# Graph convolutions: the last targets summed from gathered rows instead of a table product

## The chip, the cores and the metric

The kernel runs on one core of one Trainium2 chip. The metric is the device time of one execution in microseconds. Before the change it is 4117.46 us, the median of three runs (4089.36, 4117.46, 4130.27).

The engines are called as the profile calls them: PE (TensorE, products), DVE (VectorE), ACT (ScalarE), POOL (GpSimd) and SP (SyncE). Each executes its own instructions in their written order and waits for other engines and transfers by semaphores. Transfers are issued on the queues of SP and ACT; transfers with indirect addresses (gathers and scatters by row numbers) are issued on POOL.

## The reference

3125 nodes with 256 features, 50,000 edges sorted by target. Eight stages follow one another, and each adds to `x` what it makes of its layer-normed rows:

```python
x = x + gnn0(ln(x), edges)   # attention, 4 heads
x = x + ffn0(ln(x))          # 8 experts, top 2
x = x + gnn1(ln(x), edges)   # two attention layers
x = x + ffn1(ln(x))          # a recurrence over the rows
x = x + gnn2(ln(x), edges)   # three graph convolutions
x = x + ffn2(ln(x))          # 8 experts of width 1024, top 2
x = x + gnn3(ln(x), edges)   # one graph convolution
x = x + ffn3(ln(x))          # 8 experts of width 512, top 2
```

The change touches the convolutions of `gnn2` and `gnn3`. One layer of `gnn2` is

```python
h = h @ W
agg = segment_sum(h[src] * norm[:, None], dst)   # self loops are among the edges
h = relu(agg + b)                                # no relu after the third layer
```

with `norm = d[src] * d[dst]`, `d` the degree to the power -1/2. `gnn3` is one such layer without self loops, bias and relu.

## The kernel before, in words

**Tiles.** Nodes are cut into 25 tiles of 128 (NT = 25, padded to NP = 3200). An early part of the kernel builds a table of edges: for each pair (source tile, target tile) a 128x128 block of counts. A convolution is then dense: for each target tile, the sum over the 25 source tiles of a product of the block with the sources' rows `hs` (scaled by `d`). The blocks lie in DRAM (`ct`) as bf16, and `hs` is split into three bf16 parts (high, mid, low; `parted`, L840: two casts on POOL, L847 and L849, two differences on DVE, L848 and L850, per two tiles).

**Layers.** `gcn` (L1585) runs a whole stage. `gnn2` has three layers. The front norms `x`, multiplies by the first weight and writes `hs`. Layers 0 and 1 go through `convolve` (L1529): spans of up to four target tiles (`even_spans(4)`: seven spans, 4,4,3,4,3,4,3 tiles), and per span 25 sources x 2 halves x 3 parts = 150 products with the block as the moving operand (L1540, 128x512 or 128x384). The sums of a span lie in two PSUM tiles, with two sets of them (`accp`), and `done` takes them: DVE multiplies by the targets' `d` (L1663), ACT adds the bias with relu (L1664), PE multiplies by the next weight (L369) in what is already the next span's time, ACT scales (L1656), and `parted` makes the next `hs`. The last layer, and `gnn3`, goes through `convolve_rows` (L1546): spans of two targets, and per source and target a pair of products, L1560 (128x512: high and mid part) and L1564 (128x256: low). DVE adds the sums to `x` (L1684).

**The blocks' loads.** `table_columns` (L814) loads the blocks of one span in groups of source tiles on SP's queue (L822) into three rotating buffers (`cpool`). With self loops, POOL adds the identity to a diagonal block as soon as its group has landed (L828, `c<-c,ident`); PE's products on that block wait for it.

**The experts' fronts.** While `convolve_rows` goes on, tiles whose `x` is complete pass through the front of the next experts (`Experts.front`, L2202): norm on DVE, transposes and the gate's product on PE, choice and places on DVE (L2240 and after), again small products on PE (L2262, L2263), then two scatters of rows per tile on POOL (`slots`, L2348). `ready` gives the pieces lags in steps (a step is one target tile), and the loop writes them between the products. After CERTAIN = 20 tiles sent, `load_ahead` (L2400) starts loads for the experts.

**Order.** Within an engine the order of instructions is fixed at build time by a scheduler, which plans with its own costs of instructions. `with tc.issue_after(i)` tells it that what is written inside comes behind `i`; the engines of the two matter, as the order below shows. Gathers as such are used before the change in the attention stages only (L2023, one gather of 128 rows per 128 edges).

**Stages in time**, by the trace: up to 930 us the table, `gnn0` and its experts; 930 to 1757 `gnn1`; 1757 to 1827 the projection of the recurrence; 1827 to 2480 the recurrence; 2500 to 2755 front and layer 0 of `gnn2`; 2755 to 2984 layer 1; 2984 to 3206 the rows layer; 3206 to 3615 the experts of width 1024; 3615 to 3879 `gnn3` (rows from 3656); to the end the last experts.

The functions that the change touches, with the profile's line numbers:

## Time and profile before

| | us |
|---|---|
| median of three runs | 4117.46 |
| the profiled execution's own time | 4123.68 |
| its span in the profile | 4121.8 |
| PE busy | 3555.9 (86%) |
| DVE busy | 2155.3 (52%) |
| POOL busy | 1401.9 (34%) |
| ACT busy | 1212.7 (29%) |
| mean clock granted to PE | 0.913 of full speed |

Busy time per stage (us; DMA is the mean busy share of the 16 DMA engines):

| stretch | length | PE | DVE | POOL | DMA |
|---|---|---|---|---|---|
| 1757–1827 projection | 70 | 69.0 | 36.7 | | |
| 2500–2755 front and layer 0 | 255 | 249.3 | 57.8 | 46.4 | 0.26 |
| 2755–2984 layer 1 | 229 | 228.1 | 28.6 | 27.2 | 0.32 |
| 2984–3174 rows | 190 | 188.5 | 111.3 | 44.2 | 0.57 |
| 3206–3615 experts | 409 | 388.6 | | | |
| 3670–3879 rows of gnn3 | 209 | 206.2 | 91.6 | 38.7 | 0.52 |

How to read it: the busy share of PE is an average over the stages. In the attention stages POOL and DVE are busy too; from 2500 us on, PE is the only engine that is busy nearly all the time. In a list of events each row has start, length, engine, line, operation, `out<-in`, and in brackets the idle time of the engine before it and what ended it. In a list of waits, "who waited for it" names the engines that stood idle until the instruction was done.

### The profile page before, as it was taken

The numbers are of one execution on the slowest core, as the hardware profiler recorded it, in microseconds if no ns is written. First come the engines' busy times: TensorE is split into PE (matmuls) and PEld (weight loads), VectorE is DVE, ScalarE is ACT, GpSimd is POOL, SyncE is SP. The second block draws the span as 40 slices with busy tenths as digits, with TensorE's granted clock in tenths as the row PEclk, the third lists the DMA queues.
The fourth block names the chain that finished last, engine by engine and source line by source line (L and its number), as shares of the span: only waits on it lengthen the run. The fifth ranks groups of instructions, "written<-read, shape, count | busy, mean of one in ns | idle before, by whom it ended". The sixth has DMA issues, their size and how long they took to land. (4 is left out here: it accounts for less than half of the span.)

```text
span 4121.8 us, 72442 instructions
## 1 busy us (share of the span) xinstructions
PE 3555.9 (86%) x25990; PEld 2149.1 (52%) x26079; DVE 2155.3 (52%) x7897; ACT 1212.7 (29%) x4041; POOL 1401.9 (34%) x1321
## 2 busy tenths in 40 slices
PE   4567878676878868899999998999999999989988
PEld 3233222463222356675454455555566788856677
DVE  7567788646766645557677675111156411153411
ACT  2455333434333302114444444000100322330122
POOL 2756666444767357400000003111122222222243
PEclk8666887798989979999999999999999999989999
DMA  4444432563333254300000002333364444445465
GB/s 123 136 137 143 141 105 79 142 223 109 107 105 108 73 156 140 87 3 2 2 2 2 2 2 61 88 94 92 91 197 143 144 117 117 122 129 157 134 158 122
DMA packets 366387, 422.32 MB, mean 102 GB/s; under 512 B 44076, under 2 KB 320864, under 8 KB 362295
## 3 DMA queue, kind: packets, MB, share of 16 engines
q1 hardware_dynamic: 286833, 260.46, 21.0%
q0 software_dynamic: 62224, 140.41, 13.1%
q10 hardware_dynamic: 16950, 16.54, 1.2%
q8 instruction: 219, 3.59, 0.4%
q14 instruction: 161, 1.32, 0.1%
HBM read 337.37 MB, written 82.62 MB: 102 GB/s over the span
## 5 line engine op out<-in xcount | busy, mean ns | idle before, releaser
L2023 POOL DMA_INDIRECT edge<-scored,from x720 | 830.6, 1154 | 517.9 <-issue 238.9
L1540 PE MATMUL acc<-c,hs 128*128 128x512 bf16 (+1 forms) x2069 | 405.9, 356 | 1.7 <-POOL hs L847 0.2
L1801 PE MATMUL pz<-lstm_v,hist 128*32 128x192 f32 x7120 | 382.5, 333 | 19.3 <-DVE hist L1906 7.3
L1560 PE MATMUL acc<-hs,c 128*128 128x512 bf16 x1192 | 394.9, 379 | 0.0
L2689 PE MATMUL ph<-xt,first 128*128 128x256 f32 (+1 forms) x1624 | 351.1, 371 | 5.7 <-ACT xt L2655 3.1
L1564 PE MATMUL acc<-hs,c 128*128 128x256 bf16 x1250 | 340.6, 272 | 3.0
L2707 PE MATMUL py<-w,ht 128*128 x1484 | 337.8, 382 | 4.5 <-issue 4.1
L2082 ACT ACTIVATE edge<-edge,factor 128x65 f32<-128x65 f32 (+1 forms) x960 | 251.3, 349 | 218.8 <-DVE factor L2077 170.4
L2689 PEld LDWEIGHTS ph<-xt,first 128*128 128x128 f32 x1624 | 290.6, 196 | 41.3 <-ACT xt L2655 5.4
L1540 PEld LDWEIGHTS <-hs 128*128 128x128 bf16 x2100 | 205.6, 98 | 199.2 <-POOL hs L847 0.6
L2707 PEld LDWEIGHTS py<-w,ht 128*128 128x128 f32 x1484 | 282.9, 192 | 43.6 <-issue 5.2
L976 DVE SCALAR_TENSOR_TENSOR v<-q,g1ahv,c 128x384 f32<-128x384 f32 (+1 forms) x400 | 240.4, 646 | 112.0 <-remote 52.3
L1837 PE MATMUL pz<-pre,ident 128*128 128x192 f32 x900 | 268.4, 381 | 12.1 <-PEq L1914 11.6
L1801 PEld LDWEIGHTS pz<-lstm_v,hist 128*32 128x32 f32 x7120 | 186.0, 109 | 167.7 <-DVE hist L1906 135.9
L2348 POOL DMA_INDIRECT slots<-rows,sloti x150 | 168.5, 1123 | 307.5 <-DVE rstd L345 136.7
L2697 ACT ACTIVATE ht<-ph,first 128x256 f32<-128x256 f32 (+1 forms) x406 | 160.8, 456 | 323.2 <-PE ph L2689 284.3
L681 PE MATMUL pa<-hi,lo 128*128 128x350 bf16 (+2 forms) x600 | 166.4, 422 | 96.8 <-ACT cols L688 40.4
L1611 POOL TENSOR_TENSOR disc<-deg,expo 128x25 f32<-128x25 f32 x1 | 4.4, 4360 | 714.6 <-DVE ends L1911 714.6
L1131 PE MATMUL acc<-g1bhv,v 128*128 128x257 f32 x850 | 218.0, 407 | 25.2 <-issue 9.9
L1884 ACT ACTIVATE z<-pz 128x128 f32<-128x128 f32 (+1 forms) x900 | 176.5, 248 | 198.1 <-PE pz L1801 197.5
L2092 PE MATMUL edgeacc<-edge,hot 128*32 128x264 f32 (+1 forms) x1440 | 152.3, 468 | 82.2 <-issue 35.1
L1837 PEld LDWEIGHTS pz<-pre,ident 128*128 128x128 f32 x900 | 136.0, 190 | 149.0 <-issue 70.3
(530 smaller groups left out, 5499.2 us busy)
## 6 DMA issues: line engine op xcount, KB each, us to landing
c<-ct SPq DMA_DIRECT2D x103, 640.0 KB
c<-ct SPq DMA_DIRECT2D x75, 480.0 KB
first<-in_f_first SPq DMA_DIRECT2D x29, 1158.0 KB
slots<-slots SPq DMA_DIRECT2D x159, 130.0 KB
ct<-cols SPq DMA_DIRECT2D x12, 1600.0 KB
first<-in_f_first SPq DMA_DIRECT2D x29, 642.0 KB
edge<-scored,from POOLq DMA_INDIRECT x720
first<-in_f_first SPq DMA_DIRECT2D x29, 385.0 KB
```

What stands on the lines that cost most here:

```text
L976: nc.vector.scalar_tensor_tensor(to, q[:, h, :w], hv[:, s, h, D // nh + 1 : D // nh + 2], cols[s], op0=ALU.max, op1=ALU.mult,)
L1131: nc.tensor.matmul(a[:, : D + 1], v[0][:, j * P : (j + 1) * P], hv[:, s, 0, : D + 1], start=(s == 0), stop=(s == NT - 1),)
L1540: self.nc.tensor.matmul(acc[f][:, : n * P], lhs, cols[s], start=(s == 0 and i == 0), stop=(s == NT - 1), skip_group_check=True,)
L1560: nc.tensor.matmul(acc[t], lhs, hs[:, s, 0:2, :].rearrange("p i d -> p (i d)"), start=start, stop=stop, skip_group_check=True,)
L1564: return nc.tensor.matmul(acc[t][:, D:], lhs, hs[:, s, 2, :], start=False, stop=stop, skip_group_check=True,)
L1801: made = nc.tensor.matmul(pz[q * R : (q + 1) * R, :], s, m, start=start, stop=stop, tile_position=(0, q * R),)
L1837: made = nc.tensor.matmul(pz, self.ident, pre[:, g, s, :], start=True, stop=False)
L1884: nc.scalar.activation(three[0][:, gates, :], three[1][:, gates, :], AF.Tanh)
L2023: nc.gpsimd.indirect_dma_start(out=tile[:, g, :], out_offset=None, in_=self.rows, in_offset=bass.IndirectOffsetOnAxis(ap=index, axis=0),)
L2082: nc.scalar.mul(part, part, factor[:, g, h : h + 1])
L2689: made = nc.tensor.matmul(ph[:, m - m0, :n, :], st["w1"][:, k * hid + m * P : k * hid + (m + 1) * P], st["xt"][:, k, :n, :], start=(k == 0 ...
L2707: nc.tensor.matmul(py[:, j, :], st["ht"][:, m, j, :], st["w2"][:, m * D : (m + 1) * D], start=(m == 0), stop=(m == nhc - 1),)
```

## The change

NEAR = 4 target tiles at the end (tiles 21 to 24, FAR = 21) are no longer summed by table products. For each of their nodes the sources of its edges are listed by rank: edge number r of each of 128 targets gives one list of 128 row numbers, up to RANKS = 22 ranks. A gather by such a list brings one f32 row per target, and DVE adds the gathered rows. Edges beyond rank 22 of any of the nodes, up to 128 of them, are brought by one more gather (`more`) and put in place by one product with a 0/1 matrix (`beyond_hot`). A further fallback program runs if there are more.

Parts:

- `near_plan`, 15 pieces written between the steps of the recurrence's projection: some 90 DVE instructions, a few products on PE and five gathers on POOL (four of windows of the edge list, one of pairs). It yields the lists `ranked` and `beyond` and the matrix `beyond_hot`.
- In each layer of `gnn2` and `gnn3` the f32 rows are also stored to DRAM (`sources`, ACT's queue, before `parted`).
- `NearTiles`, below: per layer one gather `more` and 22 gathers a tile, two to a buffer of five (`got`); one addition of 128x512 per buffer on DVE; per tile a product with `beyond_hot`, additions of the own row (self loop), the three last additions and scalings. `convolve` does this for four tiles (88 gathers), `convolve_rows` for three (66 gathers; tile 21 stays in the table products, so that it has eleven spans of two).
- `near_done` takes a near tile in a `convolve` layer: two transposes on PE, relu on ACT, two products with the next weight.
- `convolve` has six spans (4,3,4,3,4,3), `convolve_rows` eleven of two.
- The fronts of the experts for tiles 22 and 23 are queued after target 12, that of tile 24 after target 18. CERTAIN is reached with 18 table targets and two near ones. `load_ahead` loads four slot rows; the wide experts load one first weight (1158 KB) ahead instead of two.

```diff
-    def convolve(self, cpool, accp, loops, hs, done):
+    def convolve(self, cpool, accp, loops, hs, done, near):
         wide = 4
-        for t0, n in even_spans(wide):
+        for t0, n in even_spans(wide, FAR if near else NT):
...
-                        self.nc.tensor.matmul(
+                        made = self.nc.tensor.matmul(
                             acc[f][:, : n * P], lhs, cols[s], start=(s == 0 and i == 0),
                             stop=(s == NT - 1), skip_group_check=True,
                         )
+                if near:
+                    near.upto(n, made.ins)
             done(t0, n, acc)
+        if near:
+            near.upto(None)
...
-        for t0, n in spans(wide):
+        for t0, n in even_spans(wide, near.first if near else NT):
...
             for lag, piece in ready(t0, n):
                 waiting.append((step + lag, piece))
+            for other in fronts.pop(t0 + n, ()) if near else ():
+                for lag, piece in ready(*other):
+                    waiting.append((step + 24 + lag, piece))
...
+                def end():
+                    self.put_rows(self.sources[layer % 2], new, t0, n)
+                    self.parted(lefts, to, new, t0, n)
...
+                def near_done(t, rows, i=i, after=after, next_layer=next_layer):
+                    turned, agg = [], aggs.tile([P, KD, P], F32, name="nearagg")
+                    def turn():
+                        pt = psum.tile([P, KD, P], F32, name="tp", padded_shape=[P, 512 // P, P])
+                        for f in range(KD):
+                            nc.tensor.transpose(
+                                pt[:, f, :], rows[:, f * P : (f + 1) * P], self.ident
+                            )
...
+                    near_tiles(i, FAR, 3.3, near_done)
...
-                if t0 + n == NT - 1:
-                    lags = [1] + [16 + j for j in range(n)] + [20, 23, 25]
+                if split and t0 + n == FAR - 1:
+                    lags = [2] + [22 + 4 * j for j in range(n)] + [34, 40, 46]
...
-                if t0 + n == CERTAIN:
-                    lags[-1] += 32
+                if experts.sent == CERTAIN:
+                    lags[-1] += 20 if split else 32
...
+                near_tiles(len(weights) - 1, FAR + 1, 3.9, near_add),
+                {12: [(FAR + 1, 2)], 18: [(FAR + 3, 1)]},
...
+class NearTiles:
+    def __init__(self, net, pool, gots, psum, rows, hs, disc, first, pace, done):
...
+        self.each = RANKS // 2
+        self.waiting, t0 = [], 5.0
+        self.more = pool.tile([P, D], F32, name="more")
+        self.put(t0, lambda: self.gather(self.more, self.net.beyond))
+        for i, t in enumerate(self.tiles):
+            state, begin = {}, t0 + i * self.each * pace
+            self.put(begin + 9.0, lambda t=t, state=state: self.begin(t, state))
+            for b in range(self.each):
+                at = begin + b * pace
+                self.put(at, self.fetch)
+                self.put(at + 9.0, lambda t=t, b=b, state=state: self.add(t, b, state))
+            self.put(at + 9.1, lambda t=t, state=state: self.end(t, state))
+
+    def gather(self, to, index):
+        with self.net.tc.issue_after(self.last):
+            self.nc.gpsimd.indirect_dma_start(
+                out=to, out_offset=None, in_=self.rows,
+                in_offset=bass.IndirectOffsetOnAxis(ap=index, axis=0),
+            )
...
+    def upto(self, n, last=None):
+        if n is None:
+            while self.waiting:
+                self.waiting.pop(0)[1]()
+            return
+        self.now, self.last = self.now + 0.325 * n, last
+        while self.waiting and self.waiting[0][0] <= self.now:
+            self.waiting.pop(0)[1]()
+
+    def add(self, t, b, state):
...
+        self.nc.vector.tensor_add(sums, self.got[n - 1] if b == 1 else sums, self.got[n])
...
-            store=True, early=6, ahead=2, more=3,
+            store=True, early=6, ahead=1, more=3,
```

`upto` counts 0.325 for a source and target, and writes a gather when its time by `pace` (3.3 or 3.9 for two gathers) has come, with `issue_after` the product just written.

The order that the build gives POOL in the changed kernel, `c` an addition of the identity (L828 before), "slots" a scatter of the experts' fronts, "cast" one of `parted`, from left to right:

```
layer 0: more, 28 gathers, c, 13 gathers, c, c, 13 gathers, 4 casts, 3 gathers, cast, c, c, c, ...
layer 1: more, 39 gathers, c, 13 gathers, c, c, 2 gathers, 4 casts, 3 gathers, cast, c, c, c, ...
rows of gnn2: more, 12 gathers, c, c, 32 gathers, c, c, 10 gathers, 4 slots, c, c, 4 slots, ...
rows of gnn3: more, 54 gathers, 8 slots, 12 gathers, slots to the end
```

On DVE the additions of gathered rows stand between the instructions of `done` and of the fronts: in layer 0 the one that takes gather 42 (the 43rd with `more`) stands before `done`'s first product of span 0, and in `gnn3` the one that takes gather 38 stands before the logits of the first front.

## The prediction

> **What bounds the kernel now.** I began with the slices of the page's section 2, since the followed chain is cut at the last gather and tells nothing.
>
> ```profile
> PE   4567878676878868899999998999999999989988
> ...
> POOL 2756666444767357400000003111122222222243
> PEclk8666887798989979999999999999999999989999
> ```
>
> One slice is 103 us. From slice 24 on (2500 us) TensorE is busy for nine tenths or more and POOL mostly for two. The stretches by time say the same for the stages that the change touches (columns: length, busy time of PE, PEld, DVE, ACT, POOL with instructions in brackets, clock, DMA share, GB/s):
>
> ```profile
> 3656.00:3760.00 104.00, 103.25 (x656) 65.72 (x669) 39.94 (x200) 4.20 (x11) 19.79 (x23) 1.00 0.52 155
> 3760.00:3879.00 119.00, 116.85 (x752) 75.28 (x766) 57.05 (x341) 5.12 (x14) 23.13 (x24) 1.00 0.48 138
> ```
>
> The convolutions are pure TensorE time at full clock: a product removed is time removed, and a product that waits is time added. What the products cost stands in the groups and in the order of events on PE:
>
> ```profile
> L1560 PE MATMUL acc<-hs,c 128*128 128x512 bf16 x1192 | 394.9, 379 | 0.0
> L1564 PE MATMUL acc<-hs,c 128*128 128x256 bf16 x1250 | 340.6, 272 | 3.0
> ```
>
> ```profile
> 2924.35 32.65 PE L1540 MATMUL acc<-c,hs 128*128 128x512 bf16 x149
> 2956.97 3.72 PE L369 MATMUL tp<-L_gnn_W,agg 128*128 128x256 f32 x16
> 2960.53 23.56 PE L1540 MATMUL acc<-c,hs 128*128 128x384 bf16 x144
> ```
>
> The mean duration overlaps its neighbours, so I take distances: a span of four targets lasts 32.65 us, one of three 23.56. In the rows stages one source takes a pair L1560 and L1564, and consecutive L1560 start 0.325 us apart (2988.17, 2988.49), so one target tile, 25 sources, is 8.1 us.
>
> The other side is POOL, where the new gathers go. The nearest row is the attention's gather of 128 rows, L2023; two of its instructions in a free run:
>
> ```profile
> L2023 POOL DMA_INDIRECT edge<-scored,from x720: 943/950/6951, 101.0 to 1718.7; - x180
> ```
>
> ```profile
> 1502.04 0.94 POOL L2023 DMA_INDIRECT edge<-scored,from  x1 [0.30 <-issue]
> 1503.29 0.95 POOL L2023 DMA_INDIRECT edge<-scored,from  x1 [0.30 <-issue]
> ```
>
> Each costs POOL 0.95 us and 0.30 us of issue: **1.25 us from one to the next**. Landing: the first four gathers of the run ended at 106.43, 111.71 and 118.42 for three groups, and DVE's waiting L2077 started at 110.28, 113.72 and 120.55; so 2.0 to 3.9 us after, I take 2. Last, the instruction that TensorE needs from POOL:
>
> ```profile
> L828 POOL TENSOR_TENSOR c<-c,ident x75: 420/427/954, 2484.9 to 3202.0; 128x128 bf16<-128x128 bf16 x75
> ...
>   DMA c<-ct: 209.9, 24
> ...
> who waited for it (us, times):
> busy tenths in 40 slices 0000000000000000000000000000000000000000
> ```
>
> It adds the self loops to a loaded table block. POOL stands waiting for the block ahead of time, and nobody ever waits for POOL. That cover is what the change uses up.
>
> **Removed.** In each of the two `convolve` layers a span of four targets goes (seven spans become six, 4 and 3 wide): 32.65 us, less what the near tiles put on TensorE: four products with `beyond_hot` (L369's 128x256 f32 form lasts 0.38) and eight transposes (about 0.25), 3.5 us; the near tiles' weight products replace equal ones. Net 29.1, twice 58.3. In each of the two rows stages three tiles go: 24.4 us, less three products of 0.38, so 23.3, twice 46.5. Together **−104.8 us**.
>
> **Moved: experts' rows earlier.** Tiles 22 to 24 pass through the fronts before the end instead of last. TensorE's waits for slots at the start of the experts were 4.9 us in 3206–3615 and 11.2 in 3879–4122. All of it may go, or none, as the scatters queue on POOL behind gathers; against it stands that f2 loads one first weight less ahead (a wait of 0 to 6 us, as no load of it is late now). I take −8, ends −16 and +6.
>
> **Hidden.** `near_plan`'s small DVE pieces go between the steps of the projection (1757–1827), where DVE is busy 36.7 of 70 us and PE 69.0; its five gathers feed only later pieces. Some 90 DVE instructions of 0.16 to 1 us, perhaps 30 us in all, fit beside, but one that waits for its gather holds the `pre` additions behind it: 1 to 8 us, I take 4. The stores of sources (ACT's queue, 3.3 MB a layer) and the gathers (11.5 MB in a `convolve` layer) come on a DMA share of 0.26 to 0.57; hidden, I take 0.
>
> **Added: gathers ahead of the self loops.** `issue_after(last)` names a product of TensorE, but the gather is POOL's; the order of the changed build shows no effect of it: gathers stand in rows ahead of the additions of `ident`. Each chain below is counted in that order, at 1.25 us, as PE's waiting instruction against when PE reaches it. PE is in order, so all products behind it wait too.
>
> Layer 0: the front paces PE until 2539; `more` can start near 2542.5, when the last source is stored. Span 0 ends near 2568. Ahead of the DVE product that frees and turns span 0's sums (L1663 in the old kernel) stands, on DVE, a sum waiting for the 43rd gather (with `more`): 2542.5 + 43×1.25 + 1.3 (three additions) + 2 = 2599.6, and DVE and ACT take 3 more (sum 0.69, products 1.07, ACT 0.47). PE wants the result 1.4 us into span 1, at 2569.4: a stall of **33 us**. The self loops of span 1, behind 42 gathers, are ready at 2596 and lie in its shadow. A later addition, behind 11 more gathers, is 5 us late. Sum 38.
>
> Layer 1: the last source of the layer before is stored about 7.3 us after the layer's first product (last product 2983.6, last cast 2990.9 in the present hand-over). `more`, 39 gathers, an addition, 13 gathers and the next addition end 7.3 + 53×1.25 + 0.8 = 74.4 us after the start; PE needs it at 41 (a span of 32.65, the hand-over, six products of source 5): 33, and 3 for a later one. Sum 36.
>
> Rows of g2: 13 gathers ahead of the first pair of additions (+5), 32 ahead of the next (40 us against a two-tile span of 16.3 and the stock in hand, +21, partly the same wait as that of front 0, whose routing on DVE stands behind those sums). Sum 28, ends 24 and 35.
>
> Rows of g3: no self loops, but front 0's routing stands on DVE behind the sum of the 38th gather. `more` starts near 3664, so that sum runs at 3664 + 39×1.25 + 2 = 3715. Today:
>
> ```profile
> 3688.24 0.17 DVE L2240 TENSOR_TENSOR logits<-tp,L_ffn_bg 128x16 f32<-128x16 f32 x1 [10.96 <-PE tp L369]
> ```
>
> and PE's products of the selection (L2262) follow at about 3692. 3716 against 3692 is 24, I take 25 with the next sum. At 1.25 us the stalls are 38 + 36 + 28 + 25 = **127 us**.
>
> **The spacing decides**: 180 gathers stand in these chains (43, 53, 45, 39), so 0.05 us on each is 9 us. The new sums are DVE instructions of two f32 inputs in SBUF, 0.69 us (L848's form), one per two gathers. In the trace such an instruction sometimes holds a gather and sometimes not: 1.47 us at 1495.25 beside a DVE product of 1.22, but 0.95 at 1517.39 beside one of 0.75. Eight such DVE instructions between 1510 and 1527 lengthened the gathers by 0.6 us in all, some 0.1 each with that of 1495. I take 1.30 us (+9). Ends: 1.25, and 1.45 (L2023's mean of 1.154 in a stage with DVE at two thirds, +36).
>
> The Trainium skill (GPSIMD Engine Reference, section 1, Specifications) states that GpSimd's SBUF interfaces are shared with VectorE and contend with DVE instructions that have two SBUF inputs. If each sum held the gathers for its whole 0.69 us, the spacing would be 1.60 and this term +63 instead of +9; the rows above show a part of it, so the measured value stands.
>
> **Sum**: −104.8 − 8 + 4 + 127 + 9 = **+27 us** on the profiled execution's 4123.7 (span 4121.8), which is 6 above the median 4117.5. Put on the median: 4144. A measurement of this kernel tells about 1% (41 us) from no change, as its three runs spread from 4089 to 4130.
>
> **Rivals.**
> *The gathers stay out of the way*, because POOL reaches them earlier than I think or the loaded blocks wait long enough: stalls of 0 to 40 us instead of 136. Then −104.8 − 8 + 4 + 25 = −84, 4034; faster. For it: POOL is busy for 46 of 255 us in layer 0, and 88 gathers need only 110 us of a layer of 200. Against it: the counted order of POOL and DVE; idle time of POOL later in the layer does not help an addition queued behind 42 gathers.
> *The gathers are dearer*: from 1.38 us apart the result is over 1% slower than before, as 27 + 180×0.08 = 41. At 1.45, +54: 4171; with landings of 3.9 us in four chains and the upper ends of rows, entry and f2 (7, 4, 14 over my values), +87: 4204. For it: the mean of L2023, and DMA shares above 0.5 in the rows stages that the gathers add to. Against it: the free run of 1.25 with DVE quiet, and DVE busy for 13 to 59% of these stages.
> *The change doesn't do what it says* in that gathers are not bound to products: that is part of the forecast; bound ones would come at 1.65 us of PE time each and the first rival's time would hold.
>
> **Chances.** Forecast, net within 1%: 0.39. First rival, faster by over 1%: 0.24. Second, slower by over 1%: 0.37, high as the forecast lies nearer to that bound. The range of the forecast itself is 4076 to 4158. The 8-in-10 range leaves a tenth at either end: 4030 (most stalls gone, as in the first rival) to 4205 (the dear case).
>
> **What will show it.** Right: PE waits on POOL's addition or on DVE's `agg` of span 0, about 33 us in one piece, once in each `convolve` layer; PE waits of some 20 us in front 0 of g2 and g3; gathers 1.25 to 1.35 us apart; layer 0 and layer 1 of g2 each longer by some 10 us than before though a span is gone. Wrong: PE without such waits (first rival), waits at f2's first weights, or stalls in the projection. I err most if the scheduler's order runs ahead of what I placed: if `more` starts 10 us sooner or later, all four chains move by 10 us each.

## The result, and the profile after

The changed kernel takes 4244.32 us (median of six runs, 4227.93 to 4253.32) against 4117.35 for the kernel before, run beside it: a ratio of 1.0316, 95% interval 1.0282 to 1.035. It is **slower by 127 us**; the forecast was slower by 27. The profiled execution took 4251.48 us, its span 4249.7.

The slices of the page of the changed kernel (each 106 us):

```profile
PE   4677887766898788999999985969879899958998
...
POOL 3767666445666366100000036354342222263243
PEclk7666888888998889999999997979889999978999
```

From slice 24 on, PE has four holes where it had none (5, 6, 7 and 5 tenths). They stand where POOL is fullest, and the granted clock is low in the same slices. So the loss is in front of TensorE, in one place per stage, as forecast; its size, and what the waits are called, is not. The groups of PE in the two `convolve` layers of the changed kernel (2497 to 3040; busy time, mean ns, then the idle time ahead of the group and what ended it):

```profile
L1734 PE MATMUL acc<-c,hs 128*128 128x512 bf16 x874 | 212.1, 390 | 61.0 <-issue 59.0 <-POOL hs L1041 0.2
L1734 PE MATMUL acc<-c,hs 128*128 128x384 bf16 x900 | 150.2, 327 | 0.3 <-issue 0.3
L373 PE MATMUL tp<-L_gnn_W,agg 128*128 128x256 f32 x168 | 50.6, 465 | 22.9 <-ACT agg L1905 22.9
```

L1734 is the old L1540 and L1905 the old L1664. The wide form has 874 records where it had 1169: the products are gone as counted. PE waits 22.9 us for `agg` (forecast: about 74 in the two layers) and 59 us for "issue", that is for nothing that the profile shows. The two rows stages look alike; the groups that answer to the old L1560 and L1564 (all from 2490 us on):

```profile
L1758 PE MATMUL acc<-hs,c 128*128 128x512 bf16 x1046 | 370.5, 396 | 43.4 <-issue 36.2 <-POOL c L1022 7.2
L1762 PE MATMUL acc<-hs,c 128*128 128x256 bf16 x1100 | 309.8, 282 | 39.0 <-issue 34.0 <-DVE sums L2436 2.2
```

So 129 us of PE's idle time is "issue". What that is shows in single events of PE in layer 1, which stands 20 us into a row of gathers there (PEld is the weight load):

```profile
2806.61 0.38 PE L1734 MATMUL acc<-c,hs 128*128 128x512 bf16 x1 [1.74 <-issue]
...
2808.02 0.38 PE L1734 MATMUL acc<-c,hs 128*128 128x512 bf16 x1 [1.04 <-issue]
2809.42 0.10 PEld L1734 LDWEIGHTS <-hs 128*128 128x128 bf16 x1 [2.72 <-issue]
2810.82 0.58 PE L1734 MATMUL acc<-c,hs 128*128 128x512 bf16 x1 [2.42 <-issue]
2812.22 0.10 PEld L1734 LDWEIGHTS <-hs 128*128 128x128 bf16 x1 [2.70 <-issue]
```

The starts lie 1.40 us apart; elsewhere in such stretches they are 0.70, 1.40 or 2.10 apart, always a multiple of 0.70 (some records are missing). Elsewhere a weight load and its product take 0.218 us together (32.65 us for 150). These **slow stretches** begin 15 to 26 us after the start of a long row of gathers and end about 6 us after the last: the rows 2540–2594, 2787–2837, 3040–3095 and 3765–3827 have stretches 2559–2599, 2805–2843, 3065–3103 and 3780–3834. The kernel before has one of 15 us, from 1496 on, at the end of a row of 32 gathers of L2023. The two gathers from which the forecast took its 1.25 us (at 1502.04 and 1503.29) lie in that stretch; of PE's pace beside them it says nothing. The stretches of time of the changed kernel (columns as before) show the clock falling with them:

```profile
2560.00:2570.00 10.00, 2.89 (x6) 0.50 (x5) 2.77 (x4) 0.00 (x0) 7.56 (x9) 0.70 0.36 105
2570.00:2580.00 10.00, 1.79 (x4) 0.42 (x4) 3.41 (x6) 0.00 (x0) 7.95 (x9) 0.50 0.35 104
3733.00:3837.00 104.00, 58.10 (x293) 36.42 (x297) 42.22 (x91) 22.38 (x55) 62.90 (x75) 0.74 0.43 132
```

The last answers to 3656:3760 of before, where PE had 103.25 of 104 us at a clock of 1.00. The gathers themselves are as forecast; two of them in the changed kernel's row of layer 0, and the group on the page:

```profile
2550.60 0.95 POOL L2393 DMA_INDIRECT got<-sources,ranked  x1 [0.30 <-issue]
2551.85 0.95 POOL L2393 DMA_INDIRECT got<-sources,ranked  x1 [0.30 <-issue]
```

```profile
L2393 POOL DMA_INDIRECT got<-sources,ranked x308 | 303.6, 986 | 178.1 <-DVE sums L2436 83.5
```

And POOL's addition of `ident` (old L828, now L1022), which nobody waited for, from the view of its line between 2490 and 3400 us:

```profile
who waited for it (us, times):
  PEld L1758: 7.6, 1
  PE acc L1758: 7.2, 1
  ACT new L1874: 5.8, 2
```

By stage, from PE's first products to the next stage's (the first `convolve` product, the first products of the two rows stages, the end): the layers 484.5 before and 531.1 after (+46.6), the rows of `gnn2` with the experts and the front behind them 671.7 and 704.5 (+32.8), the rows of `gnn3` with the last experts 466.0 and 516.8 (+50.8).

### The profile page after: what moved, and what is told of

The parts are those of the page before. It is cut to its first block, busy times and chain, and to the rows that moved or that the text cites. A ratio compares the mean times of both kernels' runs of the same rounds, so it can differ in the third digit from the quotient of the medians.

```text
span 4249.7 us, 72249 instructions
## 1 busy us (share of the span) xinstructions
PE 3518.6 (83%) x25465; PEld 2116.4 (50%) x25545; DVE 2279.9 (54%) x8175; ACT 1219.2 (29%) x4054; POOL 1709.6 (40%) x1640
## 5 line engine op out<-in xcount | busy, mean ns | idle before, releaser
L1734 PE MATMUL acc<-c,hs 128*128 128x384 bf16 (+1 forms) x1774 | 360.4, 358 | 61.3 <-issue 59.3
L1758 PE MATMUL acc<-hs,c 128*128 128x512 bf16 x1046 | 370.5, 396 | 43.4 <-issue 36.2
L2393 POOL DMA_INDIRECT got<-sources,ranked x308 | 303.6, 986 | 178.1 <-DVE sums L2436 83.5
L1762 PE MATMUL acc<-hs,c 128*128 128x256 bf16 x1100 | 309.8, 282 | 39.0 <-issue 34.0
L1734 PEld LDWEIGHTS <-hs 128*128 128x128 bf16 x1800 | 177.3, 99 | 236.8 <-issue 77.9
```

Of the source, the lines that this page charges most:

```text
L1734: made = self.nc.tensor.matmul(acc[f][:, : n * P], lhs, cols[s], start=(s == 0 and i == 0), stop=(s == NT - 1), skip_group_check=True,)
L1758: nc.tensor.matmul(acc[t], lhs, hs[:, s, 0:2, :].rearrange("p i d -> p (i d)"), start=start, stop=stop, skip_group_check=True,)
L1762: return nc.tensor.matmul(acc[t][:, D:], lhs, hs[:, s, 2, :], start=False, stop=stop, skip_group_check=True,)
L2393: self.nc.gpsimd.indirect_dma_start(out=to, out_offset=None, in_=self.rows, in_offset=bass.IndirectOffsetOnAxis(ap=index, axis=0),)
```

## The experiments

**Two kinds of chip.** The 18 runs of this section were made in five sets, each on one chip beside its own runs of the kernel before. That kernel took 4114 and 4116 us in two sets and 3940, 3940 and 3936 in three: I say chips of kind A (the result above is one) and of kind B. Differences are to the kernel before of the same set. As far as the profiles can be compared, the two kinds differ only where gathers run: from 1752 to 2474 us (the recurrence, no gathers) the changed kernel has 682.31 us of PE in 722, and nogather, with the same early code, has 683.02 in the same 722 us on kind B; the 1750 us ahead of it, with the attention stages and their gathers, are 172 us shorter on kind B. What else sets the chips apart no run shows. Stage times of the later stages of before are taken from its profile on kind A; with them the stages account for the differences on kind B within 10 us (nogather 19, as its stages ahead of the layers took longer).

Two theories. **A**: a long row of gathers itself slows TensorE (the stretches). **B**: only waits in the queues of POOL and DVE cost, as my forecast has it.

### What gathers cost by themselves

*bursts1 (kind B, a single execution).* The kernel before, with gathers that nobody needs, in three bursts of 24 to 30 in `gnn3` and one in each layer, into three buffers.

```diff
+                how = {1: {'count': 30}, 9: {'count': 30, 'parts': 32}, 17: {'count': 24, 'fill': 512}}.get(t)
+                if split and not loops and how:
+                    self.burst(bursts, x[:, t, 0:1], **how)
```

> The kernel before, unchanged in its work, with rows of extra gathers whose rows nobody reads: 30 whole rows of 128 in layer 0 and again early in the rows of g3, 30 of a quarter of the width in layer 1, 30 of 32 rows in the middle of g3's rows, and 24 whole ones with a POOL fill of about 0.5 us after each near its end. Theory A (a row of gathers by itself slows TensorE: in the changed kernel its instructions stand 0.70 us apart from about 15 gathers into a row until some 6 us after it): 0.70 us between PE instructions for about 25 us in layer 0 and in the first row in g3, 20 us lost in each, although nothing waits for these gathers; none or less in the spaced row. Theory B (only waits in queues cost): no such stretch in g3, where no addition of the identity stands on POOL, and within 10 us of the time before, apart from additions behind the rows in layers 0 and 1.

4021.27, **+81 us**. There is no slow stretch, but the rows were cut by waits for their three buffers (at most 14 gathers start within 2.5 us of one another). `gnn3` grew by 64 us, and its waits name a chain that the prediction lacks (3480 to 4020 us, waits of DVE and of PE):

```profile
DVE rows L2245 <- DMA slots<-rows,sloti: 127.0, 9, 31.0
```

```profile
PE tp L2291 <- DVE sel L2282: 54.7, 5, 19.5
```

A front of the experts ends with scatters of `slots` on POOL; the next front's first DVE instruction needs the buffer that they read. Behind a burst the scatters are late, DVE stands at that instruction in order, and PE at the choice `sel`. In the kernel before the longest of these waits is 7.2 us.

*nogather (kind B, a single execution).* The changed kernel without its gathers.

```diff
-        with self.net.tc.issue_after(self.last):
-            self.nc.gpsimd.indirect_dma_start(
...
+        return
```

> The changed kernel without its gathers in the convolutions (the sums of tiles 21 to 24 add one constant tile instead; it leaves that part of the computation out). Everything else stays: DVE's additions, the near tiles' products, the stores, the earlier fronts. Both theories: the removed products show in full, 105 us less than before and up to 16 for the earlier rows, so 4000 to 4015 us. If it stays above 4090, the cost lies in neither gathers nor what waits for them, but in the rest of the change.

3869.71, **−70.4 us**. The layers take 422.7 us, 62 less than before (forecast −58.3, with PE's waits on `agg` at 4.0); the rest from the first rows product to the end 1110.3 against 1137.7, only 27 less, where −46.5 and −8 were forecast. Waits of 14 us at the entry of the wide experts and 16 at `sel` have come in place. That the fronts of tiles 22 to 24, now earlier, press on the rows would explain the latter; no run shows it by itself.

*unread (kind A).* The changed kernel with its gathers, but sums of a constant tile, and self loops on DVE.

```diff
-                    nc.gpsimd.tensor_add(own, own, self.unit(own))
+                    nc.vector.tensor_add(own, own, self.unit(own))
...
-        self.got.append(got)
+        self.got.append(self.still)
```

> The full change with its gathers in their rows, but nobody reads what they fetch (the sums add a constant tile, so the last tiles' sums are left out) and the self loops are added on DVE, so that no instruction of PE, DVE or ACT stands behind a gather except the scatters of slots. The kernel without gathers lay 70 us below before. Theory A: PE still loses 25 to 45 us in each of four stages with no wait named, so +30 to +90 against before. Theory B: nothing is left to wait for but the slots: -70 to -40.

4371.45, **+257 us**. With nobody to hold them up the rows have 57, 67, 67 and 56 gathers. Waits of PE in layer 1 of this kernel (2790 to 3100):

```profile
PE acc L1734 <- issue: 56.3, 33, 5.0
PE tp L373 <- ACT agg L1905: 4.9, 2, 3.1
```

56 us of issue in a stretch from 2851 to 2933, beside a row from 2833 to 2917. In layer 0, though, PE also waited 44.3 us for `agg`; the expectation was wrong that nothing stood behind a gather.

*u_spaced, u_paused, u_narrow, u_few (one set, kind A)*: the unread gathers with a POOL memset behind each; with twenty memsets behind every tenth; with 64 columns in place of 256; with 32 rows in place of 128.

```diff
+        self.count += 1
+        if self.count % 1 == 0:          # u_paused: % 10 and 20 memsets
+            for _ in range(1):
+                with self.net.tc.issue_after(self.chain):
+                    self.chain = self.nc.gpsimd.memset(self.filler, 0.0).ins
```

```diff
+                out=to[:32, :], out_offset=None, in_=self.rows,
+                in_offset=bass.IndirectOffsetOnAxis(ap=index[:32, :], axis=0),
```

> The kernel with unread gathers (+257 us against before; the last tiles' sums are left out in it as in the others of this kind) with a POOL memset of some 0.54 us behind each gather, so that gathers come 1.8 us apart instead of 1.25 in rows just as long. If the rate decides: no 0.70 us stretch, and nothing is left to wait for, -70 to -20. If the number of gathers in one row decides: PE is slow for at least as long as before, +250 or more.

> The same unread gathers at 1.25 us, but after every tenth POOL clears a tile twenty times (some 11 us). The stretches began 14 to 15 gathers after the start of a row. If a row must be longer than that to slow PE: no stretch, -70 to -20. If the pause doesn't let the cause run empty: stretches from the second ten on, +100 or more.

> The unread gathers fetch 64 numbers a row instead of 256: a quarter of the bytes, as many rows (128 to a gather) and as many gathers. If the bytes slow PE: no stretches, -70 to -20. If the rows' descriptors do: as the unread kernel, +200 to +300.

> The unread gathers fetch 32 rows each instead of 128, so a quarter of the bytes and of the descriptors, in as many instructions. If descriptors or bytes slow PE: no stretches, -70 to -20. If each gather instruction does, whatever it fetches: +200 to +300, or more as POOL issues them faster.

| kernel | us, difference | layers | slow stretches from 2500 us on |
|---|---|---|---|
| unread | 4371.45, +257 | 600.2 | in every row |
| u_narrow | 4349.47, +233 | 600.8 | in every row |
| u_few | 4364.09, +248 | 600.5 | in every row |
| u_paused | 4292.01, +176 | 567.2 | none longer than 6 us |
| u_spaced | 4228.88, +113 | 528.2 | none |

Neither bytes nor rows matter: with a quarter of either, the stretches stay. A gather of 32 rows still costs POOL 895 ns, one of 64 columns 973, against 986 in the changed kernel, so the instructions came nearly as fast as before. With gathers 1.66 us apart (the memset of 0.54 us fills part of the 0.30 of issue), or with a pause of 11 us after ten, the stretches are gone. But the time fell far less than expected, for PE waited in one piece instead. Waits of PE and of DVE in layer 0 of u_spaced (2485 to 2770):

```profile
PE tp L374 <- ACT agg L1906: 49.0, 1, 49.0
```

```profile
DVE left L1043 <- POOL hs L1042: 87.5, 9, 31.6
```

The casts of the hand-over (`parted`) are POOL's, and stood behind the row; DVE waited for them, with the next span's `agg` behind it. So this set could not price the stretches.

*free_none, free, free_spaced (one set, kind B), free_again (another, kind B)*: the casts go to ACT as well, so that nothing in a `convolve` layer stands behind a gather. free_none has no gathers, free has 89 in one row in each layer, free_spaced has them some 1.7 us apart.

```diff
-            nc.gpsimd.tensor_copy(high, src[:, j : j + m, :])
+            nc.scalar.copy(high, src[:, j : j + m, :])
...
-            nc.gpsimd.tensor_copy(mid, left)
+            nc.scalar.copy(mid, left)
```

> The floor of this set: no gathers at all (the last tiles' sums are left out), sums of a constant tile, self loops on DVE and the hand-over casts on ACT, so that nothing in a convolve layer uses POOL. The kernel without gathers lay 70 us below before on another chip; the casts on ACT lengthen the fronts and hand-overs, 0 to 25 us in all: -70 to -45.

> The floor plus its gathers, fetched and never read, 89 in one row in each convolve layer; no instruction of PE, DVE or ACT in a convolve layer stands behind a gather any more, in any queue. Theory A (a row itself slows TensorE): slow from 17 us after the start of the row to 6 us after its end, PE instructions 0.70 us apart, so about 84 us lost in each convolve layer against the floor and 60 in each rows stage, +250 to +300 in all. Theory B (only waits behind gathers cost): the convolve layers as in the floor within 10 us, the rows stages up to 40 longer by the slots' scatters, +10 to +80 in all.

> The same as the kernel with free gathers, with a POOL memset of 0.5 us behind each gather (1.8 us apart, rows of 89 last 160 us). If the rate of gathers slows TensorE: no stretch of 0.70 us, and the convolve layers as in the floor within 10 us. If a row's number of gathers does, at any rate: at least the loss of the kernel with free gathers. If it is only that less comes in a given time: a loss of some two thirds.

> Gathers in rows of 89, nobody behind them in the convolve layers. On a chip of the second kind again +24 us against before and convolve layers of 423 us. On one of the first kind (theory A in its narrower form: a row slows TensorE there) the layers are 2 x 84 us longer than 423, so 590, with nearly all of PE's idle time there put down to issue, and the whole is 200 to 300 us above before.

3873.68 (−66.8), 3965.03 (+24.5), 3981.96 (+41.5); free again 3967.82 (+32). PE's products in the layers of free_none and of free:

```profile
L1734 PE MATMUL acc<-c,hs 128*128 128x512 bf16 x874 | 197.5, 379 | 2.9 <-ACT hs L1043 1.3 <-ACT hs L1041 0.3
```

```profile
L1734 PE MATMUL acc<-c,hs 128*128 128x512 bf16 x874 | 197.5, 379 | 2.8 <-ACT hs L1043 1.3 <-ACT hs L1041 0.3
```

On kind B a row of 89 gathers costs a `convolve` layer nothing: 423.0 us for both against 420.9, no slow stretch, no contention for rows or bytes. **Theory A falls as a general rule**; it is a matter of kind A. (The layers of free_spaced are 19 us longer than the floor's, without a slow stretch: the constant tile that layer 1 adds is cleared on POOL, behind the row of 150 us, and DVE's sums waited 25.8 us for it.) Of the 91 us that free takes more than its floor, 88 are in the rows stages (1213.4 against 1125.6 us), where nobody reads a gather and no self loop stands on POOL. Waits of DVE and of PE in the rows of `gnn2` of free (2749 to 3014):

```profile
DVE rows L2563 <- DMA slots<-rows,sloti: 71.4, 9, 46.6
```

```profile
PE tp L2609 <- DVE sel L2600: 50.3, 5, 40.5
```

In the floor the same two lines read 27.7 and 8.4 us. It is the slots chain of bursts1 alone, at 40 us in one piece.

### The change itself, whole and in part

*after_again (kind A), after_third (kind B)*: the changed kernel as it is. *layers (kind A)*: near tiles in the `convolve` layers alone, all 25 tiles by products in the rows stages.

```diff
-                near_tiles(len(weights) - 1, FAR + 1, 3.9, near_add),
-                {12: [(FAR + 1, 2)], 18: [(FAR + 3, 1)]},
+                None, {},
```

> The changed kernel once more, beside the kernel before on this chip. Theory A (a long row of gathers itself slows TensorE): stretches in which PE's instructions start 0.70 us apart stand again behind every row of 40 gathers, 25 to 50 us in each stage, and the ratio is again 1.028 to 1.035. Theory B (only waits in the queues of POOL and DVE cost): no such stretches are needed; then my own sum, 1.007 (+27 us), holds on a chip that shows none, with PE waits of some 30 us on POOL's addition of ident or DVE's agg in each convolve layer.

> Near tiles in the two convolve layers alone; both rows stages sum all 25 tiles as before. Theory A with the first pair of traces: the two layers cost +28 and +19, the rows nothing, so +45 against the kernel before, and the rows stages equal to before within 10 us. Theory B by my own sum: -58 + 38 + 36 = +16. If the rows were the larger part of the loss (+33 and +51 in the first traces), this one lies at least 35 us below the full change.

> The changed kernel a third time. The chips differ: where the kernel before took 4115 us, PE showed stretches of 0.70 us in rows of gathers; where it took 3940, rows of 89 gathers cost a convolve layer 2 us. On a chip of the first kind: ratio 1.028 to 1.035 as twice before. On a chip of the second kind only the waits in POOL's and DVE's queues are left, and my own sum is tested alone: +27 us, 1.007 (1.000 to 1.015), with a PE wait near 33 us in each convolve layer.

after_again 4244.44, a ratio of 1.0312 (1.0285 to 1.0339); layers 4162.57, **+48** (1.0119, 1.0086 to 1.0151), its layers at 537.8 us and its rows stages 7 us below before. So the rows stages hold 82 us of the loss on kind A. after_third 4034.76, **+99**, 1.0246 (1.0229 to 1.0263): no slow stretch, and still far above the forecast. Waits of PE in its two layers, in its rows of `gnn2` and in its rows of `gnn3` (2317 to 2825, 2825 to 3097, 3521 to 3797):

```profile
PE tp L373 <- ACT agg L1905: 76.6, 4, 35.0
...
PE tp L2605 <- DVE sel L2596: 25.8, 4, 9.3
PE tp L356 <- DVE plain L2541: 17.7, 1, 17.7
PE acc L1758 <- POOL c L1022: 7.0, 1, 7.0
...
PE tp L2605 <- DVE sel L2596: 29.5, 5, 12.8
PE tp L356 <- DVE rows L2541: 15.2, 1, 15.2
```

Here the forecast can be read term by term: 76.6 us in the layers (35.0 and 5.0 in layer 0, 31.5 and 5.1 in layer 1), 50.5 in the rows of `gnn2`, 44.7 in those of `gnn3`.

What PE waits for in the rows shows in the order of events. Most of it stands behind DVE's sums, which wait for their gathers, in order ahead of the fronts' instructions. DVE's waits in the rows of `gnn2` (2825 to 3097), and one case on DVE and on PE:

```profile
DVE sums L2436 <- DMA got<-sources,ranked: 50.8, 17, 13.7
```

```profile
2880.96 0.69 DVE L2436 TENSOR_TENSOR sums<-sums,got 128x512 f32<-128x512 f32 x1 [1.77 <-DMA got<-sources,ranked]
```

```profile
2883.11 0.66 PE L356 MATMUL tp<-ident,plain 128*128 128x128 f32 x2 [17.66 <-DVE plain L2541]
...
2884.20 0.63 PE L1758 MATMUL acc<-hs,c 128*128 128x512 bf16 x1
...
2892.48 0.38 PE L1758 MATMUL acc<-hs,c 128*128 128x512 bf16 x1
```

Of PE's 95.2 us, 35.3 in `gnn2` (17.7, 9.3, 8.3) and 35.5 in `gnn3` (15.2, 12.8, 7.5) lie behind sums in this way. The slots chain of bursts1 and free is small here: DVE's waits for `slots` come to 32.4 us in the rows of `gnn2` against 33.5 in the kernel before, and to 57.2 against 56.6 in those of `gnn3`. Only one of them, behind a row of gathers in `gnn3`, grew long, and cost PE 6.1 us:

```profile
3632.38 0.17 DVE L2559 COPY rows<-rows 128x2 f32<-128x2 f32 x1 [15.23 <-DMA slots<-rows,sloti]
```

```profile
3634.89 0.58 PE L2605 MATMUL tp<-sel,after 128*128 128x16 f32 x2 [6.07 <-DVE sel L2596]
```

The case on PE shows one more cost. Behind the wait of 17.66 us the same product takes 0.63 us at first and 0.38 later; the granted clock is 0.50 from 2883 to 2889 and 1.00 from 2891 on. So a wait costs more than its length. Without PE's waits, the layers of after_third take 426 us and its two rows stages (first to last product) 220 and 231; in nogather these are 416, 210 and 224. The mean granted clock of these stretches is 0.92, 0.88 and 0.92 against 0.99, 0.96 and 0.99.

### Versions without long rows

*paced (kind B)*: four gathers for each table block that has landed, bound behind a POOL copy of one element of that block; sums two groups later.

```diff
+            if near:
+                near.tokens[s] = nc.gpsimd.tensor_copy(near.mark, c[:, 0, 0:1]).ins
...
+        with self.net.tc.issue_after(token):
             self.nc.gpsimd.indirect_dma_start(
```

> The changed kernel with its gathers bound to POOL instructions: after each landed block of the table POOL copies one element of it, and four gathers stand behind that copy, so that they follow TensorE's progress, four in each 5 to 6 us, and the additions of the identity are never behind more than a few. Same work otherwise. Theory A and theory B both expect the waits to go: 4005 to 4035 us, faster than before by 2 to 3%. Theory A: no stretch of 0.70 us between PE instructions, as no row exceeds 8 gathers. If PE still shows such stretches, the number of gathers in flight is not what matters, and if the time stays at 4240 the gathers cost through the DMA engines themselves.

3961.15, **+21** (1.0063, 1.0042 to 1.0085), where more was expected. The layers take 474.8 us; DVE reaches sums before their gathers have landed, and PE waits 37.6 us for `agg`. From the first rows product to the end it takes 1165.4 us, 40 less than after_third, but 28 more than before and 55 more than nogather.

*paced2 (kind A)*: in the layers alone; each sum bound behind a DVE copy of one element of the block two later; seven `got` buffers instead of five. *paced3 (kind B, twice)*: the same, without sum and copy at the second block of a span, which lands just when a span's sums are to be freed.

```diff
+                    s != few and nc.vector.tensor_copy(near.seen, c[:, 0, 0:1]).ins,
...
+        if self.calls % 5 != 1:
+            with self.net.tc.issue_after(seen):
+                self.sum(self.fetched[max(0, len(self.fetched) - LAG)])
```

> Near tiles in the convolve layers alone, four gathers for each table block that has landed (bound behind a POOL copy of one element of it), and the sums bound on DVE behind a copy of one element of the block two later. Theory A: no row of more than ten gathers, so no stretch of 0.70 us; theory B: no sum waits for its gather, so DVE's agg is in time. Both: the layers' saving of the kernel without gathers (-62) less the first and last group's waits (5 to 20): -60 to -40 against before, and PE waits on agg under 5 us in a layer (17 and 20 in the first paced kernel).

> The last paced kernel (4082.6 against 4114.2) with one difference: no sum and no DVE copy of the second table block's element in a span, as that block lands just when a span's sums are to be freed, and DVE waited there (PE on agg 10.3 and 5.1 us in the two layers). Expected: those waits under 3 us in each layer, so 10 to 15 us less than that kernel: -40 to -48 against before.

> Four gathers to a landed block, in the convolve layers only. It took 72.7 us less than before on a chip of the second kind (0.9815). On one of the first kind its predecessor took 31.6 less (0.992), with 15 us of PE waits on agg that this kernel no longer has, so -40 to -50 there (0.988 to 0.990).

paced2 4082.56, **−31.6** (0.9918, 0.9891 to 0.9945), less than expected, with 15.5 us of waits on `agg`. paced3 3867.84 and 3864.96, **−72.7 and −71.0** (0.9815, 0.9796 to 0.9833; 0.9819, 0.9798 to 0.984): faster than both kernels on kind B; on kind A it was not run. PE's groups in the layers of paced3 (2318 to 2745):

```profile
L1742 PE MATMUL acc<-c,hs 128*128 128x512 bf16 x874 | 197.7, 380 | 1.5 <-POOL hs L1047 0.2
L1742 PE MATMUL acc<-c,hs 128*128 128x384 bf16 x900 | 149.5, 326 | 0.0
L374 PE MATMUL tp<-L_gnn_W,agg 128*128 128x256 f32 x168 | 39.5, 387 | 0.0
```

The layers take 422.2 us, as without any gather. In the layers the saving was there to be had; the gathers' order spent it. For the rows stages no version was found that shows as much.

## Why the prediction was wrong, step by step

| us | forecast | kind B | kind A |
|---|---|---|---|
| layers: products −58.3, stalls 38 + 36, spacing 96 of 180 gathers (4.8) | +20.5 | +23.3 | +46.6 |
| rows and experts: products −46.5, earlier rows −8, stalls 28 + 25, spacing 4.2 | +2.7 | +67.4 | +83.6 |
| ahead of the layers: `near_plan` | +4 | +8 | −2 |
| sum | +27 | +99 | +128 |

(Kind B: after_third's stages, and its 98.9 less 90.7 in the third line, so what is left over; no run takes `near_plan` out alone. Kind A: the first profiles, 127.8 in all; by the medians it is 127.)

- **Removed products: right.** In nogather the layers are 62 us shorter (forecast −58.3). From the first rows product to the end PE's time outside its waits falls by 41 us (forecast −46.5).
- **Moved rows of experts (−8): wrong.** PE's waits for slots at the experts' start fell as I thought, from 16.1 us to 4.3 in nogather and 5.5 in after_third. But other waits came in place, 16 at `sel` and 14 at the wide experts' entry, so that from the first rows product to the end PE waits 61.5 us in nogather against 47.7 before. With the products the two terms measured −27 in place of −54.5.
- **Stalls of layers 0 and 1 (74): right on kind B**, 76.6, each in one piece of 35.0 and 31.5 as named (33 and 33), through DVE's `agg` behind a sum. On kind A the same waits are 22.9 in the first profile, where PE comes late to them, and 57.0 in after_again, 40.1 of it in one piece.
- **Stalls of the rows stages (28 and 25): the step that failed.** They measured 50.5 and 44.7 on kind B. What I priced came near: the self loop 7.0 (forecast 5), front 0 behind DVE's sums 27.0 in `gnn2` (21) and 28.0 in `gnn3` (24). But I followed front 0 alone, and there are six waits in each stage. The later fronts, for which the sum had nothing, added 16.5 and 16.7: 8.3 and 7.5 behind sums that wait for further gathers, 6.1 behind the late scatters of `slots`, and 11.3 in short waits such as nogather has too, without gathers (in `gnn2` 4.4 and 3.8, there 4.4 and 3.5). I had named those scatters only in the term of −8, as a reason why it might not come.
- **What follows a wait: not in the sum.** I priced each wait at its length. The clock that falls with it goes with slower products behind it: 10 us in the layers and 20 from the first rows product to the end, after_third against nogather. The layers' total is so near to the forecast because a larger saving makes up for this: luck.
- **The rows in all.** They and the experts lie 64.7 us above the forecast on kind B: 40 are PE's waits (+88.8 us against before, where the terms 28, 25, 4.2 and −8 make +49.2), 20 are slower products behind waits, 5 a smaller saving.
- **Spacing (1.30): a little high.** The long rows of after_third run at 1.26 to 1.29 and those of the first profile at 1.26 to 1.28. The Trainium skill (GPSIMD Engine Reference, section 1, Specifications) has GpSimd and VectorE contend for SBUF where DVE reads two inputs there; these rows show at most 0.04 us a gather, not the 0.35 of a full hold.
- **Hidden gathers and stores: right on kind B**, where free's layers equal its floor's within 2 us; **wrong on kind A.** There 129 us of PE's idle time is issue, and the whole is some 28 us worse than on kind B (127 against 99). By these totals most of the issue time lies over waits that were due anyway; that is read from two kinds of chip and not shown on one. No step of the prediction had a place for it.
- **Signs.** The waits of one piece in the layers and 1.25 to 1.35 between gathers came; layers longer by 10 us each came to 12 on kind B and 23 on kind A; "PE without such waits" didn't. The rival of dearer gathers was wrong in its mechanism; that its sign held is luck. `issue_after` on PE's product did not bind POOL, as counted; binding on POOL's own copy does.

The failed step and the stretches are told apart by chips, not on one chip: the lines of the failed step are of kind B, and the result that the forecast missed is of kind A. On kind A no kernel priced the stretches without any queue wait, so their share there is a difference between kinds.

## What to carry to other kernels

Where work moves to an engine that issues in order, follow every instruction that shares its queue to the end, small scatters and casts too, and count each user that comes in turn, not the first alone. Add to a wait of the bounding engine what its clock loses by it, if the profile shows that. Spread such work by binding it to something on its own engine that already runs at the bound engine's pace (here a landed table block), and let its readers wait at a later mark of the same pace (it paid here in the layers; in the rows stages the one try cut the loss without ending it); long rows made of free issue slots cost more than they use. And take a price from the chip that it will be paid on: one and the same row cost nothing on one kind.

## What the runs showed of the hardware

- On kind A, rows of gathers at 1.25 us bring PE to one instruction per 0.70 us (or per multiple) while nothing in the profile holds it, and the granted clock to 0.50. It depends on gather instructions in unbroken sequence, not on rows or bytes; at 1.66 us apart it doesn't show. On kind B 89 in a row don't show it. The same shows in the early stages; the same products in two kernels with the same early code, the changed one on kind A and the one without gathers in the convolutions on kind B (to 1700 us):

```profile
L875 PE MATMUL pa<-hi,lo 128*128 128x350 bf16 x200 | 97.0, 485 | 70.5 <-issue 26.6 <-ACT cols L882 24.5 <-DVE hi L866 11.6
```

```profile
L875 PE MATMUL pa<-hi,lo 128*128 128x350 bf16 x200 | 97.3, 486 | 31.4 <-DVE hi L866 25.3 <-ACT cols L882 6.1
```

- The cause of these stretches stays open. PE's instruction fetches (packets of 16 KB) come about every 250 instructions of PE and PEld inside the stretches as outside, 74 us apart across the first row of the changed kernel and 21 to 34 behind it, so they follow PE's rate; that they cause it is not shown.
- A gather's cost to POOL hardly depends on what it brings: 895 ns for 32 rows of 1 KB, 973 for 128 rows of 256 B, 986 for 128 rows of 1 KB.
- Behind a wait of 17.7 us PE ran for 6 us at a granted clock of 0.50, and one form of product took 0.63 us there against 0.38 later (after_third, kind B, lines above).
